# Row loads and first weights on ScalarE's queue, token loads spread over pieces, output sums ordered after the last maxima, and a second staging ring in the output stage

## The chip, the cores and the metric

The kernel runs on one core of a Trainium2 chip. The engines are named as the profile names them: PE is TensorE (matrix products; PEld its weight loads), DVE is VectorE, ACT is ScalarE, POOL is GpSimd, and SP is SyncE, which here only issues DMAs. The metric is the device time of one execution in microseconds, and the median of three runs is given. Each engine works through its own list of instructions in order. A DMA is an instruction in such a list too: the queue that issues it first waits for what the DMA needs (a free slot, a finished store), and what stands behind it in that list waits as well. The rows SPq, ACTq and so on are these issues.

## The reference

`x` holds 2 x 2048 tokens of 2048 numbers in fp32.

```python
xn  = layernorm(x)                                   # no weights
q, k, v = split(xn @ Wqkv + bqkv)                    # 3 x 512, one head
att = softmax(q @ k.T / sqrt(512)) @ v @ Wo + bo     # over 2048 keys
s   = (xn @ Wq_w.T) @ keys.T                         # router, 64 experts
gate = softmax over the 16 largest of s, 0 elsewhere
z   = (xn @ A_w.T).reshape(64, 8) * gate             # 64 experts of rank 8
out = x + att + (z @ B_w.T) * 2
```

## The kernel before, in words

**Products.** Each fp32 operand is split into two rounded parts: `split_hi` (L122, a cast on ACT) makes the high one, `split_lo` (L125, a subtraction on DVE, at the start partly on POOL) the rest. `product` (L130) makes three matmuls of them (`PASSES`), adding into a PSUM bank; there are seven such banks, `acc()`. So a weight reaches PE in four steps: a DMA on SP's queue into a staging slot, the cast on ACT, the subtraction on DVE, the matmuls. Slots are taken in turn from rings of named memory; a slot is written again only when its last reader is done. Each DMA signals one of eight semaphores, taken in turn, so an issue also waits for the DMA eight issues before it.

**Stages.** The 4096 tokens are eight blocks of 512. (1) `first_block` does block 0: four tiles of 128 token rows are loaded (`load`), their means and variances taken (`normal`), scaled (`scale`, four quarters of 512 columns each) and transposed on PE (`turn`, L355), while the first products with V weights run (`piece`, `mul`). (2) Blocks 0 and 1 then pass the other weights (`values`, `ftile`); `norm` builds block 1's normalised operand. (3) Blocks 2 to 7 go in pairs j = 1, 2, 3 by a seven-product scheme (Strassen's in Winograd's form): `phase` runs P1, P2, P6, P5, P3, P7, P4, each of eight weight pieces, 5.46 us of PE apiece. `fetch(n + 1)` (L602) loads and splits the piece after the next into three staging slots (`r_pw`) and six split slots (`r_ph`). `beside` gives each phase other work: loads of the next token operands (`x_steps`, tile `xq`, L618) and sums and splits of them. All loads stand at the head of a phase. (4) Attention: `score`, `maxes`, `spread`, `soft`, `weigh` run as a pipeline over 8 x 16 steps. `maxes` (L951 to L963) ends a block's largest scores on DVE with the tile `mq`, which PE spreads (L973). (5) The output, `Wo` and the expert matrix together, is again made by seven products (`STEPS`) for 2 x 8 parts q: `moving` loads and splits a weight (tiles `wo`, `wb`), `stationary` sums and splits the operand (`xz`, `s`; called by `ahead`), `multiply` (L1143), `combine`, `finish`. Half way, at q = 8, the output columns change, and a second set of weights has to be in place; it is loaded during q = 7. P1's banks are copied by ACT into `u` (L1155).

**Statistics.** Blocks 1 to 7 need mean and variance ahead of their turn. `stats_steps` (L195, L212) loads token rows (tile `xs`) through a ring: three slots of 1024 columns for blocks 1 to 3 (eight loads each), two of 512 columns for blocks 4 to 7 (sixteen loads each). A load is issued one ring's length ahead of the DVE statistics that free its slot. Its steps are dealt out beside the phases: those of blocks 4 and 5 in P6 and P5 of j = 1, those of 6 and 7 in the same phases of j = 2.

**What sets the order.** The source gives one program; a scheduler merges it into one list for each engine, by the order of the text and its own estimate of when things come free. `with behind("sp")` and the like put what is inside after the instruction last noted under that name, so that it can't be scheduled ahead of it. `last["sp"]` is noted by each weight load, `last["dve"]` by each weight's subtraction, `last["pe"]` by each product, `last["act"]` by the copies into `u`.

Of the kernel before, what the change touches and what calls it, by code (L numbers as in the profile page):

```python
# [8 lines left out]
F32 = mybir.dt.float32  # L9
# [7 lines left out]
P = 128  # L17
# [46 lines left out]
def attn_ffn_kernel(ctx: ExitStack, tc, x, xT, wq, wv, wob, bqk, bv, bo, keysT, out):  # L64
# [48 lines left out]
    def behind(*keys):  # L113


        ctx_ = ExitStack()
        for k in keys:
            ctx_.enter_context(tc.issue_after(last[k].ins))
        return ctx_

    def split_hi(hi, src):
        nc.scalar.copy(hi, src)  # L122
# [78 lines left out]
    def stats_steps(i, r, cols, out):  # L201
# [5 lines left out]
        def load(k):  # L207
            if k < NT * per:
# [3 lines left out]
                nc.sync.dma_start(tiles[k], x[r0 : r0 + P, c * cols : (c + 1) * cols])  # L212
# [49 lines left out]
    def weights(src, shape, eng=None):  # L262
        ws = r_ws([P, *shape], F32, "ws")
        last["sp"] = nc.sync.dma_start(ws, src)
        wh = r_wh([P, 2, *shape], FR, "wh")
        split_hi(wh[:, 0], ws)
# [19 lines left out]
    def wv_piece(h, c2, eng=None):  # L286
        ch, cc = divmod(2 * c2, HC)
        return weights(wv[h, ch, :, cc : cc + 2, :], [2, VH], eng)
# [28 lines left out]
    def first_block():  # L317
# [5 lines left out]
        rs = const.tile([P, NT], F32, name="rs")  # L323

# [10 lines left out]
        def normal(t):  # L335
            st = const.tile([P, 4, 6], F32, name="st6", bufs=2)
            row_stats(mv[:, t, :], rows[t], 0, st)
            rstd(rs[:, t : t + 1], mv[:, t, 1:2], 1)

        def scale(t):  # L340
            for c in range(2):
                for h in range(2):
                    v = rows[t][c][:, h * 512 : (h + 1) * 512]
                    nc.vector.tensor_scalar(
                        v, v, mv[:, t, 0:1], rs[:, t : t + 1], ALU.subtract, ALU.mult
                    )

# [17 lines left out]
        def piece(c2, h, eng=None):  # L365
            return wv_piece(h, c2, eng)
# [17 lines left out]
        wh = [piece(c2, 0, nc.gpsimd) for c2 in range(2)]  # L384
# [133 lines left out]
    def ftile(i, f, xn, gx, then=None):  # L518
# [4 lines left out]
        for ch in range(2):  # L523
# [3 lines left out]
            for c4 in range(2):  # L527
                ws = w[:, 4 * c4 : 4 * c4 + 4, :]
                wh = r_wh([P, 2, 4, P], FR, "wh")
                split_hi(wh[:, 0], ws)  # L530
# [58 lines left out]
    def fetch(n):  # L589
# [14 lines left out]
        split_hi(hi, ws)  # L604
# [52 lines left out]
    def beside(j, ph):  # L657
# [91 lines left out]
    def phase(j, ph, n):  # L749

        loads, steps = beside(j, ph)
        with behind("sp"):
            for st in loads:
                st()
# [3 lines left out]
        for m, it in enumerate(ITEMS[ph]):  # L758
            ps = [acc() for t in range(NT)] if it == "V" else acc()
# [187 lines left out]
    def maxes(blk):  # L947
# [15 lines left out]
        nc.vector.tensor_tensor(  # L963
# [88 lines left out]
    def moving(p, step, kk):  # L1052


        def load():
            ws = tw[p, step, kk] = r_wo([P, 2, T], F32, "wo")
            n = 2 * p
            if step in ("P1", "P2", "P3"):
                k0, c = {"P1": (kk, n), "P2": (ND + kk, n), "P3": (ND + kk, n + 1)}[step]
                nc.sync.dma_start(ws, wob[:, k0 : k0 + 2, c, :])  # L1060
            else:
                a, b = {"P5": (0, 0), "P6": (0, 1), "P4": (1, 0), "P7": (1, 1)}[step]
                for k in range(2):
                    nc.sync.dma_start(ws[:, k, :], tw_d[p][kk + k][:, a, b, :])

        def split():
            ws = tw[p, step, kk]
            hi, lo = (r_tm[STEPS.index(step)]([P, 2, T], FR, "wb") for k in range(2))
            split_hi(hi, ws)
            split_lo(lo, ws, hi)  # L1070
# [124 lines left out]
    for s in range(NSTEP + LAG):  # L1195
# [25 lines left out]
        if e == -12:  # L1221
# [12 lines left out]
            r_wo = Ring(sb, "G9", "B29")  # L1234
# [87 lines left out]
```

## Time and profile before

| | |
|---|---|
| median of three runs | 2677.56 us (2675.84 to 2678.31) |
| profiled execution | 2676.42 us, its span 2674.6 us (1.8 us around it) |
| mean granted clock of PE | 0.993 |
| PE busy | 2636.0 us, 99% of the span |
| DVE, ACT, POOL busy | 1815.5, 859.6, 567.3 us |
| DMA | 197 GB/s over the span |

PE is idle for 38.6 us in all. About 8 of these lie before its first transposes and 4 at the very end; the others are a few single waits. "A <- B" in the list of waits means that A waited for B, with the total, the number and the longest, in us. In windows, each engine's busy time in that stretch stands with its number of instructions, then the clock that PE was granted (1.00 is full speed), the share of time in which the DMA engines were busy, and GB/s. In rows of a timeline, the start comes first, then the busy time of the instructions joined in that row, in us from the span's start.

### The profile page before, as it was taken

The page shows a single profiled execution, that of the slowest core. Times are in us where ns is not written, and L with a number is a line of the kernel's source. Part 1 is how long each engine was busy: PE and PEld are TensorE (multiplying, and loading weights), DVE is VectorE, ACT ScalarE, POOL GpSimd, SP SyncE. Part 2 cuts the span into 40 slices and gives each one's busy share as a digit, 9 for nine tenths or more (in the row PEclk, how much of TensorE's full clock was granted, in tenths as well). Part 3 has the DMA queues.
Part 4 walks back from the last instruction along what each step waited for, and adds up shares of the span by engine and source line. Part 5 has one row for each costly group of instructions (what it writes and reads, how often), then busy time and mean ns, then how long its engine had stood idle before and what let it go on. Part 6 is the DMA issues. An engine that isn't in the chain of part 4 may idle for free.

```text
span 2674.6 us, 33809 instructions
## 1 busy us (share of the span) xinstructions
PE 2636.0 (99%) x12875; PEld 2229.5 (83%) x12875; DVE 1815.5 (68%) x2481; ACT 859.6 (32%) x1271; POOL 567.3 (21%) x355
## 2 busy tenths in 40 slices
PE   8998999999999999999999999999999999999999
PEld 7888887888888888888888888888878888878887
DVE  7567737877878687756545676456657776787675
ACT  4332323333333333323233343334434222232221
POOL 2311320000000000000101111000000655566664
PEclk9999999999999999999999999999999999999999
DMA  7678764668646684536735476534457444565542
GB/s 262 218 261 300 270 248 152 216 217 284 206 143 218 227 293 146 173 118 211 290 108 189 144 268 229 208 111 142 145 182 255 159 163 162 190 211 174 178 158 103
DMA packets 243363, 530.41 MB, mean 198 GB/s; under 512 B 21577, under 2 KB 87169, under 8 KB 243201
## 3 DMA queue, kind: packets, MB, share of 16 engines
q1 hardware_dynamic: 243200, 528.26, 58.6%
q8 instruction: 101, 1.65, 0.2%
q14 instruction: 62, 0.50, 0.1%
HBM read 393.80 MB, written 134.38 MB: 197 GB/s over the span
## 4 chain that ended last, share of the span: by engine, by line
PE 91%; DVE 4%; DMA 3%; issue 1%; ACT 0%; POOL 0%; SPq 0%; DVEq 0%; ACTq 0%; POOLq 0%
PE acc L130 69%; PE acc L1143 21%; DMA xs<-in_x 1%; DMA wo<-in_wob 0%; DVE xc L254 0%; DMA pw<-in_wq 0%; DVE st L195 0%; DMA xc<-in_xT 0%; DMA xz<-oz_d 0%; DVE wb L125 0%; DMA xq<-in_xT 0%; DVE xq L645 0%; DVE wh L125 0%; DMA ws<-in_wv 0%; DVE pw L125 0%
## 5 line engine op out<-in xcount | busy, mean ns | idle before, releaser
L130 PE MATMUL acc<-t,pw 128*128 128x512 f32 x3024 | 696.7, 391 | 7.5 <-DVE pw L125 6.6
L130 PEld LDWEIGHTS acc<-t,pw 128*128 128x128 f32 x3024 | 566.9, 188 | 126.7 <-DVE pw L125 7.0
L1143 PE MATMUL acc<-wb,s 128*128 128x512 f32 x2688 | 611.7, 390 | 5.7 <-ACT u L1155 5.7
L1143 PEld LDWEIGHTS acc<-wb,s 128*128 128x128 f32 x2688 | 505.9, 188 | 111.4 <-ACT u L1155 6.2
L130 PE MATMUL acc<-ph,vt 128*128 128x512 f32 x1536 | 369.0, 391 | 0.6 <-DVE ph L125 0.6
L130 PE MATMUL acc<-qt,kt 128*128 128x512 f32 x1536 | 366.0, 389 | 0.0
L130 PEld LDWEIGHTS acc<-ph,vt 128*128 128x128 f32 x1536 | 288.3, 188 | 63.5 <-issue 1.2
L130 PEld LDWEIGHTS acc<-qt,kt 128*128 128x128 f32 x1536 | 288.1, 188 | 60.3 <-issue 0.2
L1127 POOL TENSOR_TENSOR xo<-xo,bo_bc 128x512 f32<-128x512 f32 x128 | 207.3, 1625 | 583.4 <-DMA xo<-in_x 531.1
L122 ACT CAST pw<-pw 128x1024 fp32r<-128x1024 f32 (+1 forms) x168 | 177.8, 1059 | 364.5 <-PE acc L130 267.9
L125 DVE TENSOR_TENSOR pw<-pw 128x1024 fp32r<-128x1024 f32 (+1 forms) x168 | 216.2, 1287 | 75.1 <-ACT pw L122 72.9
L130 PE MATMUL acc<-xh,wh 128*128 128x512 f32 x1152 | 263.6, 390 | 0.0
L130 PEld LDWEIGHTS acc<-xh,wh 128*128 128x128 f32 x1152 | 215.6, 188 | 45.0
L130 PEld LDWEIGHTS acc<-pw,t 128*128 128x128 f32 x2016 | 245.6, 188 | 1.2
L130 PE MATMUL acc<-pw,t 128*128 128x264 f32 x2016 | 246.1, 283 | 0.0
L122 ACT CAST s<-xz 128x1024 fp32r<-128x1024 f32 x112 | 118.1, 1054 | 368.1 <-PE acc L1143 296.7
L125 DVE TENSOR_TENSOR s<-xz,s 128x1024 fp32r<-128x1024 f32 x112 | 172.4, 1540 | 46.4 <-ACT s L122 46.3
L125 DVE TENSOR_TENSOR ph<-sp,ph 128x512 fp32r<-128x512 f32 x128 | 93.4, 732 | 121.8 <-ACT ph L122 121.0
L945 DVE TENSOR_TENSOR M<-M,sp 128x512 f32<-128x512 f32 x112 | 78.8, 704 | 122.2 <-ACT sp L939 121.7
L515 POOL TENSOR_TENSOR zt<-zt,g 128x512 f32<-128x512 f32 x24 | 37.9, 1588 | 491.5 <-DMA g<-gd 237.1
L125 DVE TENSOR_TENSOR wh<-wu,wh 128x512 fp32r<-128x512 f32 x96 | 89.7, 945 | 67.5 <-ACT wh L122 65.2
L939 ACT COPY sp<-acc 128x512 f32<-128x512 f32 x128 | 74.9, 586 | 183.3 <-PE acc L130 183.2
(147 smaller groups left out, 2379.0 us busy)
## 6 DMA issues: line engine op xcount, KB each, us to landing
vt<-v_d SPq DMA_DIRECT2D x128, 512.0 KB, 3.6
pw<-sq_d SPq DMA_DIRECT2D x72, 512.0 KB, 3.8
xz<-oz_d SPq DMA_DIRECT2D x64, 512.0 KB, 4.4
xo<-in_x SPq DMA_DIRECT2D x128, 256.0 KB, 3.5
out_y<-xo SPq DMA_DIRECT2D x128, 256.0 KB, 2.5
pw<-in_wq SPq DMA_DIRECT2D x54, 512.0 KB, 3.6
wu<-in_wq SPq DMA_DIRECT2D x48, 512.0 KB, 6.1
xq<-in_xT SPq DMA_DIRECT2D x48, 512.0 KB, 6.5
```

Of the source, the lines that this page charges most:

```text
L122: nc.scalar.copy(hi, src)
L125: return (eng or nc.vector).tensor_tensor(lo, src, raw(hi), ALU.subtract)
L130: last["pe"] = nc.tensor.matmul(ps, st(a_), mv(b_), start=first and n == 0, stop=end and n == 2)
L515: nc.gpsimd.tensor_tensor(zt, zt, gx[n], ALU.mult)
L939: nc.scalar.copy(st, ps)
L945: nc.vector.tensor_tensor(M[blk], M[blk], st, ALU.max)
L1127: nc.gpsimd.tensor_tensor(xs, xs, bo_bc[q // (NB // 2 * NH), c], ALU.add)
L1143: nc.tensor.matmul(ps, st[a_][:, kk, sl], mv[b_], start=not more and kk == 0 and n == 0, stop=kk == ND - 1 and n == 2, skip_group_check=more,)
```

## The change

It has six edits.

1. `stats_steps` issues its row loads on ACT's queue (`nc.scalar.dma_start`) instead of SP's, each after the latest weight cast noted (`last["hi"]`, new, set in `weights`, `fetch` and `ftile`). That is 24 loads of 512 KB and 64 of 256 KB.
2. `first_block` issues its first four weight pieces on ACT's queue; loads issued so do not set `last["sp"]`.
3. In `first_block`, the last quarter of `scale` is done by ACT in two operations (add the negated mean, then multiply), for which `normal` makes `nm`.
4. `phase` takes its loads as a list of groups, one group ahead of each weight piece, instead of all ahead of the first. Only P1 of j = 1 has more than one group: three of four `xq` loads.
5. In the last steps of attention, the three calls of `ahead` that prepare the output's first sums and splits are ordered behind `mq` of the last maxima.
6. For every second of the second set of output weights (`small`), `moving` stages into a second ring, `r_wo1`, of four 512-column slots, and casts and subtracts by halves. The loads of a weight are issued with its step and split one step later, where before the split came first and the next loads after it; the loads so start one step earlier.

In the lists that result, PE's order is nearly the same. SP issues 90 fewer instructions and ACT 88 row loads, 4 weight loads and some casts and scalings more. In the stage before 230 us, SP's list has three `xq` loads and one `wu` load earlier than it had.

```diff
@@ stats_steps, load
-                nc.sync.dma_start(tiles[k], x[r0 : r0 + P, c * cols : (c + 1) * cols])
+                with behind("hi"):
+                    nc.scalar.dma_start(tiles[k], x[r0 : r0 + P, c * cols : (c + 1) * cols])
@@ weights (wv_piece and piece pass eng and queue on)
-    def weights(src, shape, eng=None):
+    def weights(src, shape, eng=None, queue=None):
         ws = r_ws([P, *shape], F32, "ws")
-        last["sp"] = nc.sync.dma_start(ws, src)
+        issued = (queue or nc.sync).dma_start(ws, src)
+        if queue is None:
+            last["sp"] = issued
         wh = r_wh([P, 2, *shape], FR, "wh")
-        split_hi(wh[:, 0], ws)
+        last["hi"] = split_hi(wh[:, 0], ws)
@@ first_block
+        nm = const.tile([P, NT], F32, name="nm")
...
             row_stats(mv[:, t, :], rows[t], 0, st)
+            nc.vector.tensor_scalar(nm[:, t : t + 1], mv[:, t, 0:1], -1.0, None, ALU.mult)
             rstd(rs[:, t : t + 1], mv[:, t, 1:2], 1)
...
-            for c in range(2):
-                for h in range(2):
-                    v = rows[t][c][:, h * 512 : (h + 1) * 512]
+            for n in range(4):
+                c, h = divmod(n, 2)
+                v = rows[t][c][:, h * 512 : (h + 1) * 512]
+                if n < 3:
                     nc.vector.tensor_scalar(
                         v, v, mv[:, t, 0:1], rs[:, t : t + 1], ALU.subtract, ALU.mult
                     )
+                else:
+                    nc.scalar.activation(v, v, AF.Identity, bias=nm[:, t : t + 1])
+                    nc.scalar.mul(v, v, rs[:, t : t + 1])
...
-        wh = [piece(c2, 0, nc.gpsimd) for c2 in range(2)]
+        wh = [piece(c2, 0, nc.gpsimd, nc.scalar) for c2 in range(2)]
...
-        wh.append(piece(2, 0, nc.gpsimd))
+        wh.append(piece(2, 0, nc.gpsimd, nc.scalar))
...
-        wh.append(piece(3, 0, nc.gpsimd))
+        wh.append(piece(3, 0, nc.gpsimd, nc.scalar))
@@ beside, P1 of the first pair
-                n10[0] + n01[0] + n11[0],
+                [n10[0], n01[0], n11[0]],
@@ phase
-        with behind("sp"):
-            for st in loads:
-                st()
+        if not loads or callable(loads[0]):
+            loads = [loads]
...
         for m, it in enumerate(ITEMS[ph]):
+            with behind("sp"):
+                for st in loads.pop(0) if loads else []:
+                    st()
@@ maxes
-        nc.vector.tensor_tensor(
+        last["mq"] = nc.vector.tensor_tensor(
             mq,
@@ moving
+        small = p == 1 and STEPS.index(step) % 2 == 1
+
         def load():
-            ws = tw[p, step, kk] = r_wo([P, 2, T], F32, "wo")
             n = 2 * p
+            if small:
+                ws = tw[p, step, kk] = [r_wo1([P, T], F32, "wo") for k in range(2)]
+            else:
+                ws = tw[p, step, kk] = r_wo([P, 2, T], F32, "wo")
+                ws = [ws[:, k, :] for k in range(2)] if step not in ("P1", "P2", "P3") else ws
...
-            split_hi(hi, ws)
-            split_lo(lo, ws, hi)
+            if small:
+                for k in range(2):
+                    split_hi(hi[:, k, :], ws[k])
+                    split_lo(lo[:, k, :], ws[k], hi[:, k, :])
+            else:
+                split_hi(hi, ws)
+                split_lo(lo, ws, hi)
@@ the end of the attention loop
+            r_wo1 = mid(0, 1, 2, 3)
...
-        if e == 2:
-            load_bo(0)
-            ahead(0)
-        if e == 7:
-            ahead(1)
-        if e == 12:
-            ahead(2)
+        if e in (2, 7, 12):
+            if e == 2:
+                load_bo(0)
+            with behind("mq"):
+                ahead(e // 5)
@@ the output loop
-            m = n + 7 * q - 7 * (NG - 1) - 1
-            if 0 <= m <= 7:
+            m = n + 7 * q - 7 * (NG - 1)
+            if 0 <= m < 7:
+                more[m] = [moving(1, STEPS[m], kk) for kk in range(0, ND, 2)]
+                for load, _ in more[m]:
+                    load()
+            if 1 <= m <= 7:
                 with behind("act"):
-                    for _, split in more:
+                    for _, split in more[m - 1]:
                         split()
-                more = [moving(1, STEPS[m], kk) for kk in range(0, ND, 2)] if m < 7 else []
-                for load, _ in more:
-                    load()
```

More of the change, by code (lines that the diff above doesn't have):

```diff
@@ L121, in split_hi @@
     def split_hi(hi, src):
-        nc.scalar.copy(hi, src)
+        return nc.scalar.copy(hi, src)
     def split_lo(lo, src, hi, eng=None):
@@ L284, in values_out, with wv_piece @@
         store(v_d[i][t][:, :, at : at + VH - n0], raw(vs[:, :, n0:]))
-    def wv_piece(h, c2, eng=None):
+    def wv_piece(h, c2, eng=None, queue=None):
         ch, cc = divmod(2 * c2, HC)
-        return weights(wv[h, ch, :, cc : cc + 2, :], [2, VH], eng)
+        return weights(wv[h, ch, :, cc : cc + 2, :], [2, VH], eng, queue)
     def router_in():
@@ L363, in turn, with piece @@
                             split_lo(lo, pj, hi)
-        def piece(c2, h, eng=None):
-            return wv_piece(h, c2, eng)
+        def piece(c2, h, eng=None, queue=None):
+            return wv_piece(h, c2, eng, queue)
         def mul(ps, wh, t, c2):
@@ L529, in ftile @@
                 wh = r_wh([P, 2, 4, P], FR, "wh")
-                split_hi(wh[:, 0], ws)
+                last["hi"] = split_hi(wh[:, 0], ws)
                 last["dve"] = split_lo(wh[:, 1], ws, wh[:, 0])
@@ L603, in fetch @@
         hi, lo = (r_ph(shape, FR, "pw") for a in range(2))
-        split_hi(hi, ws)
+        last["hi"] = split_hi(hi, ws)
         last["dve"] = split_lo(lo, ws, hi)
@@ L1052, in moving @@
     def moving(p, step, kk):
+        small = p == 1 and STEPS.index(step) % 2 == 1
         def load():
-            ws = tw[p, step, kk] = r_wo([P, 2, T], F32, "wo")
             n = 2 * p
+            if small:
[3 more added lines that the diff above has]
+                ws = [ws[:, k, :] for k in range(2)] if step not in ("P1", "P2", "P3") else ws
             if step in ("P1", "P2", "P3"):
                 k0, c = {"P1": (kk, n), "P2": (ND + kk, n), "P3": (ND + kk, n + 1)}[step]
-                nc.sync.dma_start(ws, wob[:, k0 : k0 + 2, c, :])
+                if small:
+                    for k in range(2):
+                        nc.sync.dma_start(ws[k], wob[:, k0 + k, c, :])
+                else:
+                    nc.sync.dma_start(ws, wob[:, k0 : k0 + 2, c, :])
             else:
@@ L1063, in load @@
                 for k in range(2):
-                    nc.sync.dma_start(ws[:, k, :], tw_d[p][kk + k][:, a, b, :])
+                    nc.sync.dma_start(ws[k], tw_d[p][kk + k][:, a, b, :])
         def split():
@@ L1068, in split @@
             hi, lo = (r_tm[STEPS.index(step)]([P, 2, T], FR, "wb") for k in range(2))
-            split_hi(hi, ws)
-            split_lo(lo, ws, hi)
+            if small:
+                for k in range(2):
+                    split_hi(hi[:, k, :], ws[k])
+                    split_lo(lo[:, k, :], ws[k], hi[:, k, :])
+            else:
+                split_hi(hi, ws)
+                split_lo(lo, ws, hi)
             for k in range(2):
@@ L1241, in attn_ffn_kernel @@
                         part()
-        if e == 2:
-            load_bo(0)
-            ahead(0)
-        if e == 7:
-            ahead(1)
-        if e == 12:
-            ahead(2)
-    more = []
+        if e in (2, 7, 12):
[3 more added lines that the diff above has]
+                ahead(e // 5)
+    more = {}
     for q in range(2 * NG):
```

## The prediction

> **What bounds the kernel now.** I read the page's busy times and slices first, then what TensorE (PE) waited for, then windows around each long wait, then the queue or engine ahead of it.
>
> ```profile
> PE 2636.0 (99%) x12875; PEld 2229.5 (83%) x12875; DVE 1815.5 (68%) x2481; ACT 859.6 (32%) x1271; POOL 567.3 (21%) x355
> ...
> PEclk9999999999999999999999999999999999999999
> ...
> PE 91%; DVE 4%; DMA 3%; issue 1%; ACT 0%; POOL 0%; SPq 0%; DVEq 0%; ACTq 0%; POOLq 0%
> ```
>
> PE is busy 2636.0 of 2674.6 us and the change takes no product away. It can win only PE's 38.6 idle us and the half-clock time behind them. The waits of PE say where they are (total, times, longest):
>
> ```profile
> PE acc L130 <- DVE vs L125: 8.5, 1, 8.5
> PE acc L130 <- DVE pw L125: 6.6, 1, 6.6
> PE acc L355 <- DVE xs L344: 6.1, 4, 4.2
> PE acc L1143 <- ACT u L1155: 5.7, 1, 5.7
> PE misc L973 <- DVE mq L963: 3.8, 1, 3.8
> ```
>
> Five places. Windows (length, PE busy, PEld, DVE, ACT, POOL, clock, DMA share, GB/s):
>
> ```profile
> 2.00:30.00 28.00, 20.77 (x100) 15.90 (x99) 22.67 (x56) 10.75 (x41) 12.04 (x11) 0.82 0.77 256
> 224.00:230.00 6.00, 6.00 (x52) 6.00 (x51) 5.62 (x12) 1.44 (x3) 0.00 (x0) 1.00 0.86 287
> 230.00:238.00 8.00, 0.34 (x3) 0.13 (x2) 3.83 (x8) 2.13 (x8) 0.00 (x0) 0.69 0.91 309
> 395.00:405.00 10.00, 10.00 (x46) 8.28 (x45) 3.49 (x4) 1.53 (x2) 0.00 (x0) 1.00 1.04 391
> 1985.00:2009.00 24.00, 20.03 (x80) 15.46 (x78) 20.14 (x24) 7.47 (x12) 4.71 (x3) 0.93 0.75 257
> 2362.00:2374.00 12.00, 6.27 (x19) 4.70 (x19) 11.85 (x10) 4.27 (x6) 8.21 (x5) 0.72 0.79 252
> ```
>
> A wait costs more than its idle time, since the clock falls behind it. Full-clock spacing in this trace is 0.227 us for a 512-column and 0.121 us for a 264-column matmul. So 1985 to 2009 holds 80 x 0.227 = 18.2 us of work in 24.0: 5.8 lost. 2362 to 2374 holds 19 x 0.227 = 4.3: 7.7 lost. Around 230: from 224.75 to 250.18, 120 x 0.121 = 14.5 of 25.4: 10.9 lost. Around 405: from 399 to 421, 58 x 0.227 = 13.2 of 22.0: 8.8 lost. The start idles 7.2.
>
> **The change, part by part.**
>
> *(a) Start.* PE's idle 7.2 us are 4.16 for the first scaled rows, then 0.33, 0.29, 0.80, 0.78 and 0.79. Issuing the first weights on ACT puts two loads of 270 KB beside the four row chunks; before they came behind them. At 256 GB/s they take 2.1 us, so the first rows end 0 to 2.1 us later; I take 1.5, as the chunks landed evenly at 3.4 to 7.8, the sign of a full path. One scaling quarter of four (1.0 us each on DVE at 9.70) goes to ACT, tile 1's statistics (3 x 0.69) go ahead of scaling, and two weight subtractions on POOL (1.37 each) ahead of its reciprocal root, which may cost that again. The later five stalls (3.0) should mostly go, as their causes (weights, tile 1) all come earlier. Gain 1.5, ends -3 and 4.
>
> *(b) The wait at 230.* SP's queue held row loads, each waiting for a slot that DVE's statistics free, with weights behind them:
>
> ```profile
> 228.80 2.38 SPq L212 DMA_DIRECT2D xs<-in_x  x2
> 231.27 0.86 SPq L264 DMA_DIRECT2D ws<-in_wv  x2
> ```
>
> ACT's casts waited for those weights (232.16, 236.50), behind them came the copies that free the accumulators, and DVE's last subtraction at 238.39. With rows on ACT the weights go out earlier. But ACT's order becomes row load, cast, row load, cast, and only then the copies. The eighth load waits for the fifth tile's statistics (230.8), which allows copies at 231.5. DVE's subtractions come behind the seventh tile's statistics: issued at 228.80, landing 4.6 us later (as the one of 222.84 did, 227.49), 233.4, so PE starts at 234.8 instead of 238.84: 4 us. Against that, the changed order of SP puts three 512 KB `xq` and one `wu` load into this stretch that came after 251 before: 2.1 MB, 6.8 us at the 309 GB/s of a path already 0.91 busy, shared over 28 us and not all ahead of the needed tiles. I take a cost of 1 for this and count half a microsecond of clock: 3.5. Ends: -3 (all 6.8 ahead) and 8 (only 2.7 us of wait left, at full clock).
>
> The Trainium skill ("TensorE: Matmul & The Clock Gate", Part 1: The HAM clock gate) says the clock halves after an idle window of about 3.4 us; this trace agrees (1.4 us idle at 542 left it full, 4.2 us at 1997 did not). By that rule a wait of 4.5 us still pays the slow clock here, one of 2.7 would not, and the sum would rise by about 2.
>
> *(c) The wait at 405.* Twelve loads of 512 KB were ahead of the third weight piece:
>
> ```profile
> 389.08 9.54 SPq L618 DMA_DIRECT2D xq<-in_xT  x11
> 399.56 0.43 SPq L602 DMA_DIRECT2D pw<-in_wq  x1
> ```
>
> It landed at 410.2 and its halves were ready at 412.51; PE wanted it at 405.6. `phase` now spreads the loads over the first pieces: this piece stands behind four of them and waits only for a PE slot that is free by 394.7. Landing in 4 us it is early by 5. The next piece stands behind eight more loads (4.2 MB, 10.7 us at 391 GB/s): issued at 403, landed by 409, wanted with 2.3 us of splitting by 416.5. DVE's normalising of those rows starts up to 7 us later; its users come at 440. Gain 8.0 of the 8.8; ends 3 and 8.8.
>
> *(d) The wait at 1997.* DVE's chain of the last maxima has output sums and splits in between:
>
> ```profile
> 1995.80 1.23 DVE L1097 TENSOR_TENSOR xz<-xz 128x1024 f32<-128x1024 f32 x1
> 1997.06 1.14 DVE L961 TENSOR_TENSOR mhl<-m,mhl 16x32 fp32r<-16x32 f32 x1
> 1998.23 2.23 DVE L125 TENSOR_TENSOR s<-xz,s 128x1024 fp32r<-128x1024 f32 x1
> 2000.38 0.68 DVE L963 TENSOR_TENSOR mq<-mhl,pick 48x512 fp32r<-48x512 f32 x1
> ```
>
> Four sums (4 x 1.23) and the split (2.23), 7.2 us, go behind `mq`, which is then ready about 1993, before PE needs it at 1997. They come next on DVE, ahead of the subtractions for the next probabilities; 1993 + 7.2 = 1999.5 to 2000 against 1999.3 needed, so up to 1 us is left. Gain 4.8 of 5.8; ends 1 and 5.8.
>
> *(e) The wait at 2363.* ACT's copies of the accumulator stand behind two casts:
>
> ```profile
> 2366.54 1.05 ACT L122 CAST wb<-wo 128x1024 fp32r<-128x1024 f32 x1 [5.56 <-DMA wo<-in_wob]
> 2367.49 1.04 ACT L122 CAST s<-xz 128x1024 fp32r<-128x1024 f32 x1
> 2368.44 1.06 ACT L1155 COPY u<-acc 128x512 f32<-128x512 f32 x2
> ```
>
> The second ring takes away the late weight (issued 2361.10 for want of a slot). But ACT's new order has twelve weight casts instead of ten ahead of the copies, and still the cast of `s`, whose sum DVE finished at 2365.62. DVE is 11.85 of 12 us busy here, and two more subtractions (1.7 to 2.3 each) stand ahead of that sum: 2366.5, copies at 2368. Gain 0.5; ends -2 and 7.7.
>
> *(f) The pair phases* (rows of blocks 4 to 7). 64 loads of 0.33 to 0.45 us, 21 to 29 us, move to ACT, which is 18.9 of 60 us busy there (485 to 545): the issues themselves are hidden. Each also waits until statistics free one of two slots, with casts of weights and rows behind it, for which DVE and then PE wait. A slot's turn is 4.3 landing + 0.69 statistics + 0.33 issue = 5.3 us, two slots: 2.7 per load, against 3.2 in this trace (482.08 to 581.03 for 32). Casts start when PE frees their slot, two pieces (2 x 5.46) ahead, less 1.06 and 1.22 of splitting: 8.6 us of cover, of which DVE now uses up to 4.8 (cast done 511.1, subtraction 515.8). I take -0.5, ends 1.4 (the wait at 542) and -25.
>
> The rows of blocks 1 to 3 beside other phases: 16 more issues on ACT, at most 7 us, hidden under eight weight slots of 2.9 us each.
>
> The Trainium skill ("DMA: Bandwidth & Descriptors", Issuing engines are not separate DMA queues) speaks against the move: issuing from another engine saves only the time to issue. By that rule (b) is worth eight issues of 0.33, 2.6 us, and the sum falls by 1. The row at 228.80 shows more than issue time, a wait in the queue, which is why I keep mine.
>
> Sum: 1.5 + 3.5 + 8.0 + 4.8 + 0.5 - 0.5 = 17.8. The profiled execution took 2676.42 us (span 2674.6 and 1.8 around it), 1.1 under the median of 2677.56. 2676.42 - 17.8 = 2658.6; in terms of the median 2659.8, so 2660.
>
> **Rivals.**
>
> *Slower: ACT held by row loads in the pair phases.* Only (f). If statistics lag and the mean turn grows from 3.2 to p us, each of two stages loses 31p - 99 - 6, with 6 us as the middle of the cover left (3.8 to 8.6). At p = 3.8 that is 2 x 12.8 = 26 us: 2685. It decides (slower than before by 5.4) from p = 3.76. For it: DVE is 50.3 of 60 us busy there and in order, and ACT's loads stand up to three between two casts with two slots. Against: 2.7 from the rows, and loads were as serial on SP with other loads among them.
>
> *Waits move.* (b) gives nothing as the path is full, (d) only 1, (e) nothing, start nothing: 8 + 1 = 9 gained, 2668. For it: 0.91 DMA share at 230, DVE 20.1 of 24 at 1985.
>
> *Everything goes:* a 4, b 8, c 8.8, d 5.8, e 4 = 31, 2647. Against: DVE's row in (e).
>
> *No effect:* (c) gains and a lag of 3 to 5 us in each pair stage returns it: 2672 to 2683.
>
> **How the numbers follow.** Forecast (2650 to 2667) 0.50; waits move (2667 to 2672) 0.15; everything goes 0.08; no effect 0.08; slower 0.19. A measurement of this kernel can tell about 0.2%, 5.4 us. Faster 0.73, same 0.08, slower 0.19. The range, 2647 to 2686, cuts off what lies past the point p = 3.8 and half of the best case.
>
> **What would show it.** PE's waits for `pw` at 405 and `mq` at 1997 gone (c, d); that for `vs` about 4.5 us, not 8.5 (b); that for `u` still there (e); ACT's gaps in 485 to 600 named after row loads or statistics, without PE waiting (f). Wrong it would be by new waits of PE for `pw` or `t` in 480 to 600 and 795 to 900, by a first transposition later than 14.3 (11.40 before) with the later stalls kept, or by the `vs` wait longer than before.

## The result, and the profile after

| | before | after |
|---|---|---|
| median | 2677.73 us (5 runs) | 2656.96 us (5 runs, 2656.73 to 2657.57) |
| ratio | | 0.9924, 95% interval 0.9909 to 0.9938 |
| span of the profiled execution | 2674.6 us | 2655.2 us |

20.8 us less, where 17.8 were forecast (2660). The total was nearly right, but not because its terms were: the start and the stage at 230 gave 1.5 and 3.5 us less than forecast, and the stages at 405, of the maxima and of `u` gave 1.1, 1.4 and 4.6 more. These misses cancel in part, so the close total is luck. The runs below say why. Three lines of the page of the kernel after (engines' busy times, the second hardware queue, the chain that ended last):

```profile
PE 2628.8 (99%) x12875; PEld 2224.7 (84%) x12875; DVE 1807.5 (68%) x2487; ACT 863.1 (33%) x1285; POOL 569.6 (21%) x355
...
q10 hardware_dynamic: 13248, 30.45, 3.3%
...
PE 92%; DVE 4%; DMA 3%; issue 1%; ACT 0%; POOL 0%; SPq 0%; DVEq 0%; ACTq 0%; POOLq 0%
```

PE's idle time fell from 38.6 to 26.4 us (2655.2 - 2628.8). Its busy time fell by 7.2 too, with the same 12875 matmuls: fewer of them ran at a slow clock behind a wait (around the last maxima and at `u` the clock was 0.93 and 0.72, and is 1.00 in the windows below). The new queue q10 carries the 30 MB that ACT now issues. What PE waited for, after:

```profile
PE acc L131 <- DVE vs L126: 9.4, 1, 9.4
PE acc L365 <- DVE xs L351: 7.6, 3, 6.3
PE acc L1170 <- ACT u L1182: 2.6, 1, 2.6
PE misc L392 <- DVE warm L389: 1.2, 1, 1.2
PE acc L131 <- DVE t L126: 0.9, 1, 0.9
PE acc L131 <- DVE xh L126: 0.3, 1, 0.3
```

The waits for `pw` (6.6) and for `mq` (3.8) are gone; that for `u` is 2.6 instead of 5.7; that for `vs`, forecast at 4.5, is 9.4. Windows of the kernel after (length, then busy time of PE, PEld, DVE, ACT and POOL, clock, DMA share, GB/s):

```profile
220.00:226.00 6.00, 6.00 (x52) 6.00 (x51) 3.94 (x7) 0.68 (x2) 0.00 (x0) 1.00 1.00 350
226.00:230.00 4.00, 3.34 (x28) 3.13 (x26) 2.07 (x4) 1.39 (x3) 0.00 (x0) 1.00 1.04 416
230.00:234.00 4.00, 0.00 (x0) 0.00 (x0) 3.47 (x7) 1.09 (x2) 0.00 (x0) 1.00 1.02 395
...
1978.00:2002.00 24.00, 24.00 (x104) 19.10 (x104) 23.72 (x35) 10.33 (x19) 8.62 (x3) 1.00 0.93 315
...
2345.00:2357.00 12.00, 9.44 (x42) 7.51 (x41) 12.00 (x11) 4.86 (x6) 11.25 (x7) 1.00 0.65 219
```

Around the last maxima PE no longer stops: 104 matmuls in 24 us against 80. At `u` 42 matmuls stand in 12 us instead of 19, and the clock stays at 1.00: an idle time of 2.56 us did not slow it here. Before 230 the DMA path is now full, at 350 to 416 GB/s, as feared; what that did to the weights is read below.

The two waits that went can be read in the lists. SP's queue after, where the weight piece (`pw`) now stands between token loads (`xq`); it was issued at 399.56 before:

```profile
391.29 2.12 SPq L628 DMA_DIRECT2D xq<-in_xT  x3
395.68 0.34 SPq L612 DMA_DIRECT2D pw<-in_wq  x1
...
396.79 6.53 SPq L628 DMA_DIRECT2D xq<-in_xT  x8
404.00 1.70 SPq L612 DMA_DIRECT2D pw<-in_wq  x2
```

And DVE's chain of the last maxima after, without sums in between, `mq` ready at 1983.6 and used by PE at 1985.4 without a wait:

```profile
1982.66 0.18 DVE L973 TENSOR_TENSOR mhl<-m,mhl 16x32 fp32r<-16x32 f32 x1
1982.88 0.69 DVE L975 TENSOR_TENSOR mq<-mhl,pick 48x512 fp32r<-48x512 f32 x1
1983.49 1.21 DVE L126 TENSOR_TENSOR s<-xz,s 128x1024 fp32r<-128x1024 f32 x1
```

**Stage lengths.** All kernels have 12875 matmuls in nearly the same order, so the start of the n-th one can be set beside the n-th of another, and the differences are lengths of stages. These are the lengths, in us, in the profiled execution of each kernel; the experiments are explained below.

| kernel | start (to 168th) | 230 (1200 to 1320) | 405 (2040 to 2100) | 542 (2700 to 2850) | rest of pairs (2850 to 4950) | maxima (9900 to 10060) | `u` (11500 to 11640) |
|---|---|---|---|---|---|---|---|
| before | 37.98 | 25.28 | 22.71 | 31.00 | 383.70 | 43.23 | 39.71 |
| c_alone | 36.06 | 27.39 | 13.60 | 34.10 | 383.67 | 43.58 | 38.98 |
| d_alone | 35.86 | 26.60 | 23.01 | 29.50 | 383.68 | 37.25 | 40.07 |
| e_all | 38.29 | 28.77 | 22.84 | 30.90 | 383.67 | 43.01 | 37.07 |
| e_ring | 37.02 | 26.13 | 22.48 | 30.41 | 383.67 | 42.92 | 32.67 |
| after | 37.02 | 26.82 | 13.60 | 31.06 | 384.16 | 37.00 | 34.59 |
| rows_sp | 37.22 | 27.67 | 13.60 | 30.51 | 383.61 | 36.99 | 34.24 |
| xq_late | 37.14 | 27.04 | 13.60 | 30.03 | 384.42 | 37.00 | 34.65 |
| first_w_sp | 34.53 | 26.71 | 13.60 | 30.41 | 384.14 | 36.98 | 35.67 |
| vs_first | 37.12 | 23.24 | 13.60 | 30.87 | 383.98 | 36.98 | 34.34 |
| vs_copy | 36.83 | 19.32 | 13.60 | 30.80 | 384.37 | 36.99 | 38.40 |
| one_act | 37.16 | 28.34 | 13.60 | 38.11 | 417.41 | 37.00 | 35.51 |
| one_sp | 36.56 | 26.11 | 13.60 | 33.00 | 398.99 | 37.04 | 34.66 |
| best | 33.47 | 19.75 | 13.60 | 30.32 | 384.46 | 37.01 | 33.75 |

The first five kernels have the same code up to 300 us. Their lengths at the start (35.86 to 38.29) and at 230 (25.28 to 28.77) show how much a stage that DMAs feed differs from execution to execution, 2.4 and 3.5 us; so there the means of several kernels are compared, and one pair of profiles shows little. The stages at 405 and of the maxima repeat within 0.7 us. All ratios below are to the kernel before, with its 95% interval.

### The profile page after: what moved, and what is told of

It reads as the page before. It is cut to its first block, busy times and chain, and to the rows that moved or that the text cites. A ratio compares the mean times of both kernels' runs of the same rounds, so it can differ in the third digit from the quotient of the medians.

```text
span 2655.2 us, 33831 instructions
## 1 busy us (share of the span) xinstructions
PE 2628.8 (99%) x12875; PEld 2224.7 (84%) x12875; DVE 1807.5 (68%) x2487; ACT 863.1 (33%) x1285; POOL 569.6 (21%) x355
## 4 chain that ended last, share of the span: by engine, by line
PE 92%; DVE 4%; DMA 3%; issue 1%; ACT 0%; POOL 0%; SPq 0%; DVEq 0%; ACTq 0%; POOLq 0%
PE acc L131 69%; PE acc L1170 22%; DMA xs<-in_x 2%; DVE st L196 1%; DMA ws<-in_wv 1%; DMA xc<-in_xT 1%; DVE pw L126 1%; DVE xc L256 1%; DVE xq L655 1%; DVE wh L126 0%; DVE xc L257 0%; DVE t L126 0%; DVE wb L126 0%; DVE xs L351 0%; DVE s L126 0%
```

## The experiments

My theory after the result: the stages are independent, each edit has its own stage; the token loads (c), the order behind the maxima (d) and the output ring (e) gain; the move of row loads to ACT gains nothing at 230. The rivals: the row loads' move is needed for the other gains, or (as recorded) gains itself.

**c_alone: before, with the token loads in groups only.**

```diff
-                n10[0] + n01[0] + n11[0],
+                [n10[0], n01[0], n11[0]],
@@ phase
-        with behind("sp"):
-            for st in loads:
-                st()
+        if not loads or callable(loads[0]):
+            loads = [loads]
...
         for m, it in enumerate(ITEMS[ph]):
+            with behind("sp"):
+                for st in loads.pop(0) if loads else []:
+                    st()
```

> The kernel before with only the grouping of token loads in the phases. If the stages are independent, PE's wait for the third weight piece (6.6 us at 405.6, 8.8 us with the slow clock) goes and nothing else moves: 9.1 us less than before, 2668.6 us, and from 420 us on every matmul is 9.1 us earlier. If the gain in the whole change needed the row loads off SP's queue as well, part of the wait stays: 2671 to 2675 us.

2667.5 us against 2676.7, ratio 0.9964 (0.9951 to 0.9977). The stage at 405 fell from 22.71 to 13.60, which is 60 matmuls at 0.227: all that was lost there, 9.1 us. PE's waits in c_alone, of which that for `pw` is gone and the others are still there:

```profile
PE acc L130 <- DVE vs L125: 10.5, 1, 10.5
...
PE acc L1145 <- ACT u L1157: 5.2, 1, 5.2
PE misc L975 <- DVE mq L965: 3.7, 1, 3.7
...
PE acc L130 <- ACT t L122: 1.5, 1, 1.5
```

So this gain needs nothing of the row loads' move. The new wait for `t` (the split token operand, at 534) and its slow clock took 3.1 us back at 542. Whether the later token loads cause it isn't settled, as the stage takes 30.0 to 31.1 in the later kernels, which have the same grouping (one_act and one_sp aside).

**d_alone: before, with the output's first sums behind the last maxima only.**

```diff
-        if e == 2:
-            load_bo(0)
-            ahead(0)
-        if e == 7:
-            ahead(1)
-        if e == 12:
-            ahead(2)
+        if e in (2, 7, 12):
+            if e == 2:
+                load_bo(0)
+            with behind("mq"):
+                ahead(e // 5)
```

> The kernel before with only the output's first sums ordered behind the last maxima. The recorded step says 4.8 us with up to 1 us of wait left; the comparison of the two profiles says 6.6 us. Independent stages: 2671.1 us, PE's wait for mq gone and no new one before 2010 us. Rival: the sums now end too late for the next stage and 2 us or more come back at the first output products: 2673 us or more.

2671.5 us, ratio 0.9977 (0.9967 to 0.9987). The stage of the maxima went from 43.23 to 37.25, 6.0 us, and the output stages that follow are not longer. The sums are not missed later.

**e_all and e_ring: before, with the second ring and early loads, and with the ring alone.** In e_ring only `moving` and the ring differ; the order "split the weight before, then load the next" stays. In e_all the weight of step m is loaded first and that of step m - 1 split behind it:

```diff
+            r_wo1 = mid(0, 1, 2, 3)
@@ moving
+        small = p == 1 and STEPS.index(step) % 2 == 1
...
+            if small:
+                ws = tw[p, step, kk] = [r_wo1([P, T], F32, "wo") for k in range(2)]
...
@@ the output loop, in e_all alone
-            m = n + 7 * q - 7 * (NG - 1) - 1
+            m = n + 7 * q - 7 * (NG - 1)
...
```

> The kernel before with only the second staging ring and its loads one step earlier. The recorded step says 0.5 us, as the sum ahead of the last cast of s was thought to be late by DVE's load; the two profiles say 5.2 us. If the ring is the cause: 2672.5 us and PE's wait for u about 2.6 us instead of 5.7 at full clock. If the 5.2 us came from the other edits (another phase between PE and DVE after 14 us less in front), 2677 us.

> The kernel before with the second ring alone: four half slots for every second weight, but each weight still loaded only after the one before it is split. If the number of slots is what held back the weights, most of the gain is here: about 2673 us. If the loads have to be issued a step earlier too, the weights come as late as before: 2676 to 2678 us, with PE's wait for u at 5 us or more.

e_all: 2672.4 us, 0.9982 (0.9973 to 0.9992); its stage went from 39.71 to 37.07. e_ring: 2670.4 us, 0.9977 (0.9966 to 0.9987); its stage went to 32.67, 7.0 us less, where 140 matmuls at 0.227 are 31.8. I had expected that most of the gain needs the ring, but not that the early loads might take part of it back. How much they take is not clear: e_all's profile is the slowest of its ten executions and e_ring's the fastest of its eight, the medians differ by 2.0 us, and the intervals overlap. ACT in e_all, where the cast of `s` waits 9.4 us for its sum on DVE and `u` stands behind it:

```profile
2368.80 1.04 ACT L122 CAST s<-xz 128x1024 fp32r<-128x1024 f32 x1 [9.40 <-DVE xz L1110]
2369.75 1.07 ACT L1170 COPY u<-acc 128x512 f32<-128x512 f32 x2
```

And in e_ring, where `s` and the copies wait for PE only and PE no longer waits for `u`:

```profile
2356.73 1.06 ACT L122 CAST s<-xz 128x1024 fp32r<-128x1024 f32 x1 [4.43 <-PE acc L1158]
2359.46 0.59 ACT L1170 COPY u<-acc 128x512 f32<-128x512 f32 x1 [1.67 <-PE acc L1158]
2362.13 0.59 ACT L1170 COPY u<-acc 128x512 f32<-128x512 f32 x1 [2.08 <-PE acc L1158]
```

With early loads the scheduler puts more subtractions of weights ahead of that sum: from the 11200th matmul on there are ten in e_all and in the kernel after, and eight in e_ring and in the kernel before. With the ring alone the sum (`xz`) runs at 2353.85; counted from the 11500th matmul it starts after 4.4 us, against 13.2 in the kernel before and 12.7 in e_all. DVE is as busy in the 35 us ahead of the copies as in the kernel before (30.72 us from 2319 to 2354, against 31.05 from 2327 to 2362), so it wasn't DVE's load that made the sum late.

**rows_sp and xq_late: after, with the row loads back on SP's queue; after, with the early `xq` loads held back.**

```diff
# rows_sp
-                with behind("hi"):
-                    nc.scalar.dma_start(tiles[k], x[r0 : r0 + P, c * cols : (c + 1) * cols])
+                if True:
+                    nc.sync.dma_start(tiles[k], x[r0 : r0 + P, c * cols : (c + 1) * cols])
# xq_late
-        split_lo(vs[:, 1, n0:], v[:, n0:VH], vs[:, 0, n0:])
+        last["vs"] = split_lo(vs[:, 1, n0:], v[:, n0:VH], vs[:, 0, n0:])
...
-            with behind("sp", "pe"):
+            with behind("sp", "pe", *(["vs"] if i else [])):
                 for st in todo.get(k, []):
```

> The changed kernel (2657.0 us) with the row loads back on SP's queue; all other edits stay. My recorded step said that moving them gains 3.5 us at 230 us and costs 0.5 us in the pair phases; the two profiles say that it cost 1.5 us at 230 and about 1 us in all later. Theory: with rows on SP the wait at 230 is 8.5 us as before and the time 2654.5 to 2656. Rival (recorded): the move helped, as SP's weights stand behind rows: 2660 us.

> The changed kernel, but the four token loads that came into the stretch before 230 us (and ran at a DMA share of 1.0 from 212 to 234) are held until the copies of block 1's second half of V are made. Theory DMA: the weights and rows in the stretch then land sooner, PE's wait for vs falls from 9.4 to about 4.5 us as in the recorded step: 2652 us. Rival order: what holds PE is that ACT and DVE have all rows' statistics and eight casts ahead of the copies; the wait stays at 8 us or more: 2656 to 2658 us.

rows_sp: 2656.8 us, 0.9925 (0.9910 to 0.9940), the same as after, and outside both expectations (2654.5 to 2656, and 2660). xq_late: 2656.6 us, 0.9926 (0.9909 to 0.9943), the same too, but this run tests nothing: its four early `xq` loads were issued at 210.1 to 219.0 us, as in the kernel after (209.6 to 218.6), and the DMA share stayed at 1.00 to 1.03 from 212 to 234. The added order held nothing back.

The stage at 230 has a mean of 26.8 us in the five kernels with the old code there, 27.2 in the four with rows on ACT and copies unchanged (after, xq_late, first_w_sp, one_act) and 26.9 in the two with rows on SP (rows_sp, one_sp): no difference beyond the spread. But two things differ between these groups. In the kernels with rows on SP only one `xq` load comes early (in rows_sp at 219.5, the others from about 250 on), and about 300 GB/s are moved, as before. So the rows on ACT's queue and the earlier token loads, together, leave the stage as long as it was; what each does alone was not measured.

What the two did to the weights can be read. This is the fifth weight of the next half, first in the kernel before, then in the one after: its issue, and its cast, which waits for it last.

```profile
226.99 0.38 SPq L264 DMA_DIRECT2D ws<-in_wv  x1
232.16 0.63 ACT L122 CAST wh<-ws 128x528 fp32r<-128x528 f32 x1 [6.32 <-DMA ws<-in_wv]
...
223.94 6.96 SPq L266 DMA_DIRECT2D ws<-in_wv  x3
233.05 0.63 ACT L123 CAST wh<-ws 128x528 fp32r<-128x528 f32 x1 [2.59 <-DMA ws<-in_wv]
```

It was issued 3.05 us earlier, took 9.1 us instead of 5.2, and was cast 0.9 us later. The time from issue to cast is 5.2 to 5.9 us in all seven kernels with rows on SP, and 9.1 to 11.0 in after, xq_late and first_w_sp. So the full path did cost time: what the earlier issue gained, the slower landing gave back.

In the pair phases (2700 to 4950) rows_sp is 1.1 us shorter than after. About half of that lies in the part that repeats (383.61 to 383.70 with two slots and rows on SP, 383.98 to 384.46 with rows on ACT); the rest lies in the stage at 542, which varies by more than that.

**vs_first and vs_copy: after, with work ordered behind the copies that empty the accumulators.** In vs_first block 2's rows and statistics, in vs_copy also the casts and subtractions of later weights:

```diff
# both
-        split_lo(vs[:, 1, n0:], v[:, n0:VH], vs[:, 0, n0:])
+        last["vs"] = split_lo(vs[:, 1, n0:], v[:, n0:VH], vs[:, 0, n0:])
@@ values
-                    with behind("sp", "pe", "dve"):
+                    with behind("sp", "pe", "dve", "vs"):
                         steps[c2]()
# vs_copy
-        last["hi"] = split_hi(wh[:, 0], ws)
-        last["dve"] = split_lo(wh[:, 1], ws, wh[:, 0], eng)
+        with behind(*after):
+            last["hi"] = split_hi(wh[:, 0], ws)
+            last["dve"] = split_lo(wh[:, 1], ws, wh[:, 0], eng)
...
-                wh = wv_piece(h, c2)
+                wh = wv_piece(h, c2, after=["vs"] if h and c2 >= 2 else ())
```

> The changed kernel, but block 2's row loads and statistics are ordered behind the copies that empty the accumulators of the first half of V. Theory order: the copies no longer stand behind seven tiles of rows, PE's wait at 230 goes (under 1 us) and so does the slow clock: 10 to 12 us less, 2645 to 2647 us, unless the statistics are then late for the next stage, which would show as a new wait between 250 and 330 us. Theory DMA: the weights are late whatever the order; at least 4 us of wait stay: 2652 us.

> As the kernel with block 2's rows behind the copies, and also the casts and subtractions of the third and later weights of the second half of V ordered behind those copies; their loads are not. Ordering the rows alone left 6.4 us of wait, with casts of later weights ahead of the copies. If that order is all that is left, PE's wait for vs is under 1 us and the time 2657.0 - 10 to 12 = 2645 to 2647 us. If the weights' landing is the bound (DMA share 0.9 to 1.0 there), PE waits for wh instead of vs and the time is 2650 to 2654 us.

vs_first: 2653.0 us, 0.9908 (0.9893 to 0.9923); the stage 23.24 and the wait 6.4. ACT in vs_first, its copies of V (`vs`) behind casts of the next half's weights, each waiting for its DMA:

```profile
231.54 0.63 ACT L123 CAST wh<-ws 128x528 fp32r<-128x528 f32 x1 [1.20 <-DMA ws<-in_wv]
233.46 1.29 ACT L123 CAST wh<-ws 128x528 fp32r<-128x528 f32 x2 [1.29 <-DMA ws<-in_wv]
...
234.72 0.37 ACT L123 CAST vs<-acc 128x248 fp32r<-128x248 f32 x1
```

vs_copy: 2650.5 us, 0.9902 (0.9885 to 0.9918); the stage 19.32 and the wait 3.0. Its ACT, with one such cast left ahead of the copies:

```profile
230.68 0.63 ACT L123 CAST wh<-ws 128x528 fp32r<-128x528 f32 x1 [2.46 <-DMA ws<-in_wv]
...
231.28 0.37 ACT L123 CAST vs<-acc 128x248 fp32r<-128x248 f32 x1
```

Together the two orders make the stage 7.5 us shorter, of the 12.3 that it loses (26.8 - 14.5). With them it takes 19.32 us, and 19.75 in best below; in the eleven kernels with neither it takes 25.28 to 28.77. PE has seven accumulators, the next half needs one of the first half's four, and the copies that free them were listed, on ACT and on DVE, behind work for later that waited for its own transfers. On DVE the order can be read directly. In the kernel after, its last subtraction of V starts 2.8 us after ACT's copy, with statistics of later rows in between; in vs_first (last line) it starts 0.7 us after it:

```profile
235.56 0.37 ACT L123 CAST vs<-acc 128x248 fp32r<-128x248 f32 x1
...
237.14 1.27 DVE L196 BATCH_NORM_STATS2 st<-xs 128x6 f32<-128x512 f32 x2
238.33 1.04 DVE L126 TENSOR_TENSOR vs<-acc,vs 128x248 fp32r<-128x248 f32 x3
...
235.41 1.05 DVE L126 TENSOR_TENSOR vs<-acc,vs 128x248 fp32r<-128x248 f32 x3
```

But both orders also hold back transfers. In vs_first five row loads are gone from the stretch, and in vs_copy the held casts keep their slots, so that two weight loads go out later too: from 230 to 234 the DMA share is 0.68 and 0.17, against 1.02 in after. How much of the 7.5 us comes from the order and how much from the thinner traffic isn't separated. Neither run met the order theory's expectation of under 1 us of wait, and both times lie near what was written down for late weights (2652, and 2650 to 2654), though in vs_copy PE still waits for `vs` and not for a weight. The 3.0 us left stand behind one weight that lands late. The two runs' total times overlap; only the stage tells them apart.

vs_copy lost 3.8 us again at `u` (38.40 against 34.59), where PE waited 3.5 us for `wb`. Its profile is the slowest of its four executions (2654.24; the others 2648.35 to 2650.50), so this may belong to that execution; why it happened I did not follow up.

**first_w_sp: after, with the first four weights on SP's queue.**

```diff
-        wh = [piece(c2, 0, nc.gpsimd, nc.scalar) for c2 in range(2)]
+        wh = [piece(c2, 0, nc.gpsimd) for c2 in range(2)]
```

(and the same for the third and fourth)

> The changed kernel with the first four weight pieces back on SP's queue; the order of scaling and ACT's share in it stay. In the profile of the change PE's first transposition came 2.8 us later and the later stalls went; together 1 us earlier. If the loads beside the rows cost those 2.8 us, the first transposition is at 12 us and the time 2655 to 2656.5. If the weights on SP are late for the first products, it is 2657 to 2659.

2655.4 us, 0.9920 (0.9905 to 0.9935). In the total that isn't clear of the kernel after, in the stage it is: the start takes 34.53 us instead of 37.02 (36.6 to 37.2 in all seven kernels with the weights on ACT). PE's first transposition starts at 11.46, as before (11.40), where after has 14.21. DVE's list says where these 2.75 us come from. Its last statistics of tile 0, two of tile 1 and the scaling of tile 0, in the kernel after:

```profile
8.60 0.69 DVE L196 BATCH_NORM_STATS2 st<-xs 128x6 f32<-128x512 f32 x1 [0.65 <-DMA xs<-in_x]
...
11.00 1.28 DVE L196 BATCH_NORM_STATS2 st<-xs 128x6 f32<-128x512 f32 x2 [1.16 <-DMA xs<-in_x]
...
13.63 1.43 DVE L351 TENSOR_SCALAR xs<-xs,mv,rs 128x512 f32<-128x512 f32 x3
```

And the scaling in the kernel before, then in first_w_sp:

```profile
9.70 4.01 DVE L344 TENSOR_SCALAR xs<-xs,mv,rs 128x512 f32<-128x512 f32 x4 [0.76 <-POOL rs L189]
...
9.74 3.56 DVE L351 TENSOR_SCALAR xs<-xs,mv,rs 128x512 f32<-128x512 f32 x3 [0.76 <-POOL rs L190]
```

With the weights on ACT, tile 0's last statistics come only 0.85 us later (7.75 in first_w_sp), and the scale factor is ready at 10.54 instead of 9.71. But the scaling then waits until 13.63, because the scheduler put statistics of tile 1 ahead of it, and these wait for their own rows. In first_w_sp the scaling comes first again, so this run undoes both things at once. The loads beside the first rows thus cost about 0.85 us directly, and the order that came with them most of the rest. What the new start gains elsewhere (the later stalls of PE sum to 1.4 us in after, 3.0 before) makes up for it: the start stage has a mean of 37.0 us with the old start and with the new.

**one_act and one_sp: one staging slot for the row loads of blocks 4 to 7, on ACT's and on SP's queue.** The recorded rival, made true.

```diff
-    r_xr = half(7, 8)
+    r_xr = half(7)
```

> The changed kernel with one staging slot instead of two for the row loads of blocks 4 to 7, so that each load waits for the statistics of the one before it: the recorded rival made true. One slot's turn by the rows of the trace is 5.3 us a load against 3.2, for 32 loads in each of two stages. By the recorded formula ACT is held 31 x 5.3 - 99 - 6 = 59 us in each stage, 118 us in all: 2775 us. If the casts don't really stand behind the row loads, or the cover is far larger, it stays below 2700.

> The same single slot, but with all row loads on SP's queue. If what costs is that ACT is held (its casts), SP's queue takes the wait instead and only the weights' loads stand behind it, which have three staging slots: well below the version on ACT, by 30 us or more. If what costs is that DVE, in order, waits for each row tile, or that the loads' pace is the bound whichever queue holds them, both take the same time within 10 us.

one_act: 2696.4 us, 1.0076 (1.0056 to 1.0096). one_sp: 2678.9 us, 1.0017 (1.0007 to 1.0027). By the medians that is 39 and 22 us more than the kernel after. In the profiles the pair phases (2700 to 4950) take 455.5 and 432.0 us, where after takes 415.2: 40.3 and 16.8 us more; but one_act's profile is the slower of two executions and one_sp's the fastest of eight, so the medians are the better measure. The loads' pace is nearly the same, 4.3 us (486.88 to 619.98 for 32) and 4.5 (472.83 to 611.49), so about 17 us are due to the queue that holds the wait. Neither expectation for one_sp fits (30 us or more apart, or within 10), and one_act stays far under the 2775 us of the recorded formula. ACT in one_act between 470 and 900 us:

```profile
ACT pw L123 <- PE acc L131: 91.2, 32, 6.2
ACT pw L123 <- DVE st L196: 39.0, 9, 7.3
ACT pw L123 <- DVE mv L199: 22.5, 5, 6.4
```

The casts of weights wait for statistics (`st`, `mv`), with which they have nothing to do, because a row load stands ahead of them. In one_sp no such line is among the longest. But PE in one_act hardly waits for weights:

```profile
PE misc L235 <- POOL mr L190: 25.4, 4, 9.9
...
PE acc L131 <- DVE yv L750: 3.5, 2, 2.9
```

and in one_sp:

```profile
PE misc L235 <- POOL mr L190: 10.7, 4, 3.6
```

It waits for the statistics' last result `mr`, which it transposes itself; presumably this small transposition stands in PE's own list where the scheduler took the statistics to be done, but that was not tried. So the path to PE that the rival named (weights cast late) was not the one that cost most: the loss was real, but it came mainly through the late end of the statistics.

**best: vs_copy, with the first weights on SP's queue and the output ring without early loads.**

> The kernel of the run before (rows and later weights ordered behind the copies) with two parts of the change undone as well: the first four weights back on SP's queue, and the second set of output weights loaded only after the split before, in the second ring. If the three are independent: 2657.0 - 7 (wait at 230, 3.0 instead of 9.4 us) - 2.5 (start) - 2 (no wait for u) = 2645.5 us. If the start's gain is given back at the wait at 230, as a DMA path that is full there would, 2648 us; if the ring alone no longer suffices behind an earlier start, PE's wait for u or wb of 2 us or more is back and it is 2648 to 2650.

2644.9 us (2644.5 to 2646.0), ratio 0.9888 (0.9872 to 0.9905): 30 us less than the kernel before (2675.15 us beside it), and 12 less than the change by the profiled spans, 10 by the ratios. PE's longest waits in it:

```profile
PE acc L131 <- DVE vs L126: 3.7, 1, 3.7
PE acc L366 <- DVE xs L352: 3.6, 2, 2.8
PE acc L1171 <- DVE s L126: 1.4, 2, 1.2
```

The parts keep their gains together: the start 33.47, the stage at 230 19.75, the one of `u` 33.75.

## Why the prediction was right or wrong

The forecast of 17.8 us met 20.8, with these terms:

| step | forecast | measured, by stage | from |
|---|---|---|---|
| (a) start | 1.5 | 0 (mean 37.0 and 37.0) | first_w_sp: -2.5 with the weights on ACT, +2.5 for the rest |
| (b) 230 | 3.5 | 0 (26.8 and 27.2) | rows_sp, vs_first, vs_copy (xq_late tests nothing) |
| (c) 405 | 8.0 | 9.1 | c_alone |
| (d) maxima | 4.8 | 6.2 | d_alone |
| (e) `u` | 0.5 | 5.1 | e_ring, e_all |
| (f) pairs | -0.5 | -0.5 (384.16 against 383.70) | rows_sp, one_act |

That sums to 19.9; the two profiled spans differ by 19.4.

**(a)** The term that was mis-sized is tile 1's statistics ahead of the scaling. The forecast gave them 3 x 0.69 = 2.1 us and set them against the quarter that goes to ACT; it left only the rows' later landing, 1.5 us, as a loss. Measured, the rows' statistics came 0.85 us later, but the scaling then stood 3.1 us behind tile 1's statistics (10.54 to 13.63), which waited for rows of their own. The first transposition came 2.75 us later than in first_w_sp, at 14.21, just short of the 14.3 that was named as a sign of being wrong. That the later stalls go was right for about half: 1.4 of 3.0 us stayed. Gain and loss cancel. (Of the idle time before the change, 5.4 us lie before the first transposition, 1.19 and 4.16; about 8 is the sum over the whole start.)

**(b)** The step that failed: "I take a cost of 1 for this", the price of the fuller path, and with it the "copies at 231.5" from which "PE starts at 234.8" follows. The weights did go out earlier, but the fifth took 9.1 us to its cast instead of 5.2, and in ACT's list casts that waited for weights and row loads that waited for statistics stood behind each other. The eighth row load was issued at 234.51, behind statistics that the forecast had at 230.8; the copies came at 235.56; the seventh tile's statistics, forecast for 233.4, ran from 237.14, and DVE's subtraction behind them from 238.33. PE started at 238.78, against 238.84 before. I saw the order ("row load, cast, row load, cast, and only then the copies") and still counted only one row's wait. vs_first and vs_copy show that 7.5 us go when that work stands behind the copies; how these divide between the order and the transfers that it holds back stays open, since xq_late did not hold its loads back. The sign of being wrong that the forecast had named, a wait for `vs` longer than before, was there as well (9.4 against 8.5), though the wait differs between executions of the same code (10.5 in c_alone).

**(c)** Right. The piece was issued at 395.68 (forecast 394.7) and nothing of the wait was left; I had kept 0.8 us as a reserve that wasn't needed.

**(d)** Right in its mechanism; the up to 1 us of remaining wait didn't come. The forecast put four sums next on DVE, ending at 1999.5 to 2000 (1993 + 7.2 is 2000.2); in the kernel after only one of them (1985.22) ran ahead of the next probabilities, and the others stood from 2010.61 on. The small wait for `ph` behind it went too.

**(e)** The step that failed: "two more subtractions (1.7 to 2.3 each) stand ahead of that sum: 2366.5, copies at 2368". Set back by the 14.2 us that the kernel after is ahead there, the cast of `s` ran at 2364.3 and the copies at 2365.3, against 2367.49 and 2368.44 before. The two subtractions did stand ahead, yet the copies were 3.2 us earlier, the idle time was only 2.56 us, and the clock stayed full. I took DVE at 11.85 of 12 us as a sign of overload. It was a backlog: weights that came late piled up in one place. In e_ring, with as much work on DVE, the sum comes in time and PE no longer waits for `u`. My reason may hold for one half of the edit: early loads do put more work ahead of the sum. Their cost is not well known. It is 4.4 us between the two profiles and 2.0 between the medians, and in the changed kernel the stage takes 34.2 to 35.7 us with early loads (38.4 in vs_copy) and 33.75 without, in best.

**(f)** Right, -0.5 forecast and measured; but the -0.5 was taken and not worked out, so that the size agrees is partly luck. Row loads turned in 2.8 us each (485.32 to 572.73 for 32), against a forecast of 2.7. In 470 to 600 us ACT's casts of weights waited 14.1 + 6.3 us behind rows, the longest 6.5, and PE waited only 0.9 us there, for `t`, as before: that is inside the cover of up to 8.6. The rival's formula gives 2 x (31 x 4.3 - 105) = 57 us for one_act's pace, measured 39; it had the pace wrong (4.3, not 5.3) and the path to PE too.

**The rules of the Trainium skill.** "DMA: Bandwidth & Descriptors", Issuing engines are not separate DMA queues, speaks of issue time only as the gain of a second queue. By rows_sp the move, with the token loads that came earlier with it, gained nothing at 230 (27.2 us against 26.9), closer to that rule than to my row. "TensorE: Matmul & The Clock Gate", Part 1, has an idle window of about 3.4 us; the 2.56 us at `u` agree with it (clock 1.00 in the window above), but the last section shows a shorter idle time that was followed by the slow clock and a longer one that was not, and here the measurement decides. In the prediction's own trace the two idle times set beside that rule are 0.90 us at 542, not 1.4, and 3.82 us at 1997, not 4.2, which is that of the weight loads.

## What to carry to other kernels

When PE stops for a free accumulator, look at what stands ahead of the copies that empty it, on each engine that takes part, and try that work behind them; here the stage became 7.5 us shorter, together with the transfers that this held back, while a second queue, with the earlier loads that came with it, changed nothing. When an edit is to hold something back, read in the trace that it did. An engine that is full just ahead of a wait may only be working off what came late: ask when its inputs came, before taking its load as the bound. And a DMA issued by a compute engine brings its wait along: with two slots nearly all of it was hidden, with one the kernel took 39 us longer, against 22 on a queue that computes nothing.

## What the runs showed of the hardware

Between 2.1 and 3.7 us, the length of PE's idle time alone does not tell in these runs whether the clock falls behind it. In first_w_sp 2.11 us (from 2345.76 on) were followed by half clock, for 3.41 us from 2347.72 on; in best 3.70 us (225.86 to 229.56) were not. The windows behind the two, with the clock after POOL's busy time, first_w_sp first:

```profile
2348.00:2352.00 4.00, 4.00 (x11) 3.18 (x12) 4.00 (x4) 3.14 (x4) 3.99 (x3) 0.61 0.51 165
...
230.00:234.00 4.00, 4.00 (x35) 4.00 (x34) 1.72 (x5) 0.89 (x2) 0.00 (x0) 1.00 0.58 191
```

Half clock also followed 2.16 and 2.36 us in one_sp, 2.90 in one_act and 2.99 in vs_copy, and did not follow 2.31 in vs_first, 2.56 in the kernel after and 2.60 in one_sp. What decides is not shown here.

And a DMA path that moves more can be slower for the one load that is waited for. Before 230 the kernel before moved 287 and 309 GB/s in the windows shown, at a share of 0.86 to 0.91, and the fifth weight took 5.2 us from issue to cast; the kernel after moved 350 to 416 GB/s, at 1.00 to 1.04, and it took 9.1.
